# Reordering the opening of the first top-p attention: tile 0's logits through two PSUM names, its search ahead of a diffusion sum

## The chip, the cores and the metric

The kernel runs on one core of a Trainium2 chip. A core has five engines that run their own instruction streams[...]: TensorE (PE in the profile; PEld is its weight load), VectorE (DVE), ScalarE (ACT), GpSimd (POOL) and SyncE (SP), which here issues the DMAs. The metric is the device time of one execution in microseconds (us), the median over runs.

## The reference, cut to what matters

Four graph layers are applied in turn to `x`, 3327 nodes by 256 features, each followed by a residual and a normalization. The fourth is the one that the change touches. It runs two steps; each step computes a sparse attention from the current features and applies two operators:

```
q = X @ W1.T @ W2.T ;  k = X @ W3.T          # 64 features each
probs = softmax(q @ k.T)                      # N x N, row by row
A = probs, row-sparsified to the smallest set of largest entries whose
    sum reaches 0.9 (top-p), then divided by its row sum
R = (adj + I) / row sum
Xf = R @ Xf        # "diffusion"
Xa = A @ Xa        # "attention"
Z += Xf @ U1[n].T + Xa @ U2[n].T
```

For each row the kernel so needs: its 3327 logits, their exponentials and total, the threshold at which the sorted exponentials reach 0.9 of the total, and then two products with a 3328 x 3328 matrix.

## The kernel before, in words

Rows are padded to 3328 and cut into 26 tiles of 128 rows (`nt`). In the first attention (`p = 0`) tiles are worked in 13 pairs. Four things are made for each tile:

- **Logits**, `scores` (L1141): four groups (`c0` in steps of `KC` = 416). A group is two matmuls into a PSUM tile `sc` of two banks (L1148 to L1154), and a copy by ScalarE into `e`, the tile's 128 x 3328 row buffer (L1160; L1163 for the last group, whose halves differ in width). `sc` has one buffer, so a group's matmuls wait for the copy of the group before. The last column of `e` is filled by GpSimd (L1146).
- **Search**, `search_short` (L1387): VectorE takes the eight largest of each of 26 segments of `e` (MAX8 into `cand`), ranks them in six rounds (`top`, `rest`), ScalarE turns `e` into exponentials and their total (L1404) and later the 48 ranked ones (L1408), VectorE finds the threshold `v` and zeroes what lies below it in two halves of `e` (the two 128 x 1664 operations), and adds up what is kept (`kept`). It is a Python generator with 14 stops; `looks(k)` (L1688) advances the search at the head of a queue by `k` stops.
- **Diffusion sum**: tile 0's is made in layer 2; tile 1's by `diffused_first` (L1210): 26 matmuls of X against tiles `at` of the adjacency, which arrive in DMAs of 8, 8, 8 and 2 blocks (L1217), and one VectorE operation (`with_own`, L1207) that moves the sum out of PSUM into `F`. From tile 2 on, `diffused_pair` (L1224) makes two tiles at once with seven products in place of eight; each part of two column blocks needs three DMAs (L1230 to L1232) and one VectorE subtraction into `cb` (L1234). The buffers `at` are three.
- **Attention product**, `attended_pair` (L1252): TensorE transposes both tiles' `e` (`tp`), ScalarE copies them (`wt`, L1263), VectorE forms sums (`sw`), TensorE multiplies.

`own_part` (L1203) on GpSimd scales a tile's own rows before a diffusion sum is added. `blocks` (called at L1670) prepares differences of X in `G` with four VectorE operations at the beginning.

In this part `fixed` is true: TensorE's and VectorE's operations are kept in the order in which the Python code records them (helper at L891, which is why most lines of the profile read L891). ScalarE's, GpSimd's and SyncE's instructions are placed by the scheduler of the tile framework, and each engine then runs its own in that order. `stage` (L1692) interleaves the diffusion of a later pair with logits and looks; `attend_to` (L1706) finishes the queue of searches before a pair's transposes.

The beginning, ahead of the first `stage`, is what is changed:

```
groups = logits(0)
x = diffused_first(quads, psum, 1, xfs)
for _ in groups:
    next(x)
queue.append(searches[0])
spread = spreading(1)
groups = logits(1)
for _ in x:
    next(groups, None)
    looks(2)
```

So one group of tile 0's logits alternates with four products of tile 1's diffusion sum; then tile 0's search starts, with two looks for each further stop of the sum.

Of the kernel before, what the change touches and what calls it, by code (L numbers as in the profile page):

```python
# [9 lines left out]
F32 = mybir.dt.float32  # L10
# [8 lines left out]
P = 128  # L19
# [27 lines left out]
KC = 416  # L47
# [3 lines left out]
def gnn_kernel(ctx: ExitStack, tc: tile.TileContext, n: int, a: dict, out: bass.AP):  # L51
    nc = tc.nc
# [6 lines left out]
    small = ctx.enter_context(tc.tile_pool(name="small", bufs=4))  # L59
# [4 lines left out]
    eps_t = consts.tile([P, 1], F32, name="eps_t")  # L64
# [112 lines left out]
    with tc.tile_pool(name="l1b", bufs=1) as wpool, tc.tile_pool(name="l1at", bufs=2) as l1at:  # L177
# [62 lines left out]
        with tc.tile_pool(name="l1aw", bufs=1) as cwork, tc.tile_pool(name="l1c", bufs=2) as ch, \  # L240
# [61 lines left out]
            def plan(c):  # L302


                if c == 0:
                    return dict(project={g + 1: (g,) for g in range(NG)}, taps={7: (0,), 8: (1,), 9: (2, 3)}, gates={5: (0, 1), 6: (2,)},
                                silu=9, mixed=10, sizes={10: (0, 1), 11: (2, 3)}, exps=(11, 12), log=13)
                return dict(project={5: (0, 1), 6: (2, 3)}, taps={7: (0, 1), 8: (2, 3)}, gates={7: (0, 1), 8: (2, 3)},
                            silu=8, mixed=9, sizes={9: (0,), 10: (1, 2), 11: (3,)}, exps=(11, 12), log=13)
# [42 lines left out]
            banks = {0: ["y0", "y1", "y2", "ps"], 1: ["y3", "ps"]}  # L352
# [125 lines left out]
            def quota(c, s):  # L478


                k = c * DS + s
                n = next((x for x in range(2, nch) if k < due(x - 1)), None)
                if n is None:
                    return 24
                if k < due(0):
                    return 0
                if n not in shares:
                    busy = [duty(*divmod(i, DS)) for i in range(due(n - 2), due(n - 1))]
                    more = TILE * tiles_of(n)
                    level = max(busy) + more  # L490
                    while sum(max(0, level - x) for x in busy) > more:
                        level -= 1
                    shares[n] = [max(0, level - x) for x in busy]
                return TILE * starts[n] // P + sum(shares[n][:k - due(n - 2) + 1]) + AHEAD - taken
# [246 lines left out]
            for k, (c, s) in enumerate(states):  # L741
# [5 lines left out]
                p = plan(c)  # L747
# [55 lines left out]
                if c and 9 <= s < 9 + tiles_of(c - 1):  # L803
                    rs, nb = plus[:2]
                    i = s - 9
                    x = X[:, starts[c - 1] // P + i, :]
# [20 lines left out]
                q = quota(c, s)  # L827
# [38 lines left out]
    half = nt // 2 * P  # L866
    nseg = npad // SEG
    with tc.tile_pool(name="l3", bufs=1) as pool, tc.tile_pool(name="l3d", bufs=1, space=DRAM) as dram:
# [135 lines left out]
        with tc.tile_pool(name="l2c", bufs=1) as cpool:  # L1004
# [5 lines left out]
            with tc.tile_pool(name="l2a", bufs=1) as wpool, \  # L1010
                    tc.tile_pool(name="l2p", bufs=3, space=PSUM) as psum:

                q = cpool.tile([P, nt], F32, name="q")
# [124 lines left out]
        def in_order(op):  # L1138
            return lambda *x, **k: tc.keep_in_program_order(op(*x, **k))  # L1139

        def scores(work, psum, p, q, e):  # L1141


            copy = in_order(nc.scalar.copy) if p else nc.scalar.copy
            if npad > n:
                nc.gpsimd.memset(e[:, n:], NEG)  # L1146
            halves = e.rearrange("p (h c) -> p h c", h=2)
            for c0 in range(0, half, KC):  # L1148
                pl = psum.tile([P, 2, 512], F32, name="sc", bufs=1)
                ws = [min(KC, n - c0 - h * half) for h in range(2)]  # L1150

                for h, w in enumerate(ws):
                    k = slice(h * DA, (h + 1) * DA)
                    mm = tensor.matmul(pl[:, h, :w], q[k, :], kT[p][k, c0:c0 + w], start=True, stop=True)  # L1154
                    if p:
                        here(mm)
                if p:
                    yield
                if ws[0] == ws[1]:
                    copy(halves[:, :, c0:c0 + ws[0]], pl[:, :, :ws[0]])  # L1160
                else:
                    for h, w in enumerate(ws):
                        copy(halves[:, h, c0:c0 + w], pl[:, h, :w])  # L1163
                yield
# [45 lines left out]
        def diffused_first(quads, psum, it, out):  # L1210

            own_part(it)
            acc = psum.tile([P, 2, 512], F32, name="acc")[:, 0, :D]
            for j0 in range(0, nt, 4 * JQ):
                m = min(4 * JQ, nt - j0)
                at = quads.tile([P, 5, JQ, P], F32, name="at", bufs=3).rearrange("p k j r -> p (k j) r")
                nc.sync.dma_start(at[:, :m, :], a["adjT"][it][:, j0:j0 + m, :])  # L1217
                for j in range(m):
                    tensor.matmul(acc, at[:, j, :], X[:, j0 + j, :], start=(j0 + j == 0), stop=(j0 + j == nt - 1))
                    if j % 4 == 3 or j == m - 1:  # L1220
                        yield
            with_own(acc, it, out)

        def diffused_pair(quads, psum, i, b, out):  # L1224

            def part(j0):
                m = min(JQ, nh - j0)
                at = quads.tile([P, 5, JQ, P], F32, name="at", bufs=3)
                rows = [a["adjT"][2 * i + r].rearrange("p (h j) r -> p h j r", h=2)[:, :, j0:j0 + m, :] for r in range(2)]
                nc.sync.dma_start(at[:, :2, :m, :], rows[0])  # L1230
                nc.sync.dma_start(at[:, 2, :m, :], rows[1][:, 1])
                nc.sync.dma_start(at[:, 3:, :m, :], mixed[i][:, :, j0:j0 + m, :])  # L1232
                cb = quads.tile([P, 2, JQ, P], F32, name="cb", bufs=2)
                vector.tensor_tensor(cb[:, :, :m, :], at[:, 3:4, :m, :].to_broadcast([P, 2, m, P]), at[:, :3:2, :m, :], op=ALU.subtract)  # L1234
                a11, a12, a22, s2, s4, s1, s3 = (x[:, k, :m, :] for x, y in ((at, 5), (cb, 2)) for k in range(y))
                return a11, a12, s1, a22, s2, s3, s4

            for r in range(2):
                own_part(2 * i + r)
            pa = psum.tile([P, 2, 512], F32, name="acc")  # L1240
            ahead = part(0)
            yield
            for j0 in range(0, nh, JQ):
                w, ahead = ahead, part(j0 + JQ) if j0 + JQ < nh else None
                for j in range(min(JQ, nh - j0)):
                    products(pa, j0 + j, [x[:, j, :] for x in w], b)
                    yield
            c = assembled(quads, pa)
            for r in range(2):
                with_own(c[:, r, :], 2 * i + r, out)  # L1250
# [401 lines left out]
        with tc.tile_pool(name="l3w", bufs=2) as work, tc.tile_pool(name="l3s", bufs=4) as sm:  # L1652


            def start(p, t, es, searches, search):
                if p or t:
                    q = work.tile([2 * DA, P], F32, name="q")
                    nc.sync.dma_start(q, qd[p][t])
                else:
                    q = q0  # L1660
                es[t] = work.tile([P, npad], F32, name="e", bufs=4)
                searches[t] = search(work, sm, es[t], *(x[p][:, t:t + 1] for x in (tots, vs, kepts)),
                                     **({"halves": True} if p and t == nt - 1 else {}))
                return scores(work, psum, p, q, es[t])

            with tc.tile_pool(name="l3p", bufs=2, space=PSUM) as psum, tc.tile_pool(name="l3a", bufs=1) as quads:
                fixed = True
                es, searches, xfs, todo, queue = {}, {}, [xf0], [], []
# [3 lines left out]
                def look():  # L1672
                    while queue and next(queue[0], queue) is queue:
                        queue.pop(0)
# [5 lines left out]
                def logits(t):  # L1680
                    return start(0, t, es, searches, search_short) if t < nt else iter(())

                def spreading(i):
                    x = diffused_pair(quads, psum, i, b, xfs) if i < nh else iter(())
                    next(x, None)
                    return x

                def looks(k):  # L1688
                    for _ in range(k):
                        look()  # L1690
# [30 lines left out]
                        next(todo[r][0])  # L1721
                    ends[0] = todo[0][0]

                groups = logits(0)
                x = diffused_first(quads, psum, 1, xfs)
                for _ in groups:
                    next(x)
                queue.append(searches[0])
                spread = spreading(1)
                groups = logits(1)  # L1730
                for _ in x:
                    next(groups, None)
                    looks(2)
                for _ in groups:
                    pass
                queue.append(searches[1])
# [27 lines left out]
                for it in (nt - 2, nt - 1):  # L1764
                    for _ in range(7):
                        acc = next(values)
# [4 lines left out]
                    acc = next(values)  # L1771
# [19 lines left out]
            with tc.tile_pool(name="l3q", bufs=3, space=PSUM) as psum, tc.tile_pool(name="l3at", bufs=3) as atp, \  # L1791
                    tc.tile_pool(name="l3b", bufs=2) as lone:
                es, searches, xfs = {}, {}, []
# [4 lines left out]
                for i in range(-2, nt + 1):  # L1798
                    def search(t):
                        if 0 <= t < nt:  # L1800
                            next(searches[t])

                    values, logits = iter(()), iter(())
                    if 0 < i:
                        values = attended(lone, psum, es[i - 1], G, 3, in_order(nc.scalar.copy))
                    if i + 2 < nt:
                        logits = start(1, i + 2, es, searches, search_long)
# [196 lines left out]
```

## Time and profile before

| | |
|---|---|
| time, median of 3 runs | 3408.01 us (3407.56 to 3412.42) |
| the profiled execution's own time, and its span | 3412.8 us, 3411.0 us |
| PE, DVE, ACT, POOL busy over the span | 92%, 79%, 51%, 33% |
| layer 2's last product ends, first logits start | 1700.9 us, 1701.8 us |
| first transposes of the first pair complete | about 1758 us |
| stretch 1701 to 1757: PE, DVE, ACT, POOL busy | 35.95, 39.60, 17.43, 20.15 of 56 us |
| stretch 1757 to 2570 (rest of the first attention): PE busy | 795.56 of 813 us |

A row of the timeline gives start, duration, engine, line, operation, output and input tiles, the shapes, how many instructions are merged into it, and in brackets how long the engine had been idle before it and what ended the wait. A line L891 is the helper's, so rows are told apart by their tiles. An fp32 matmul of the program shows as two records, so "x8" is four matmuls. PEclk is the share of TensorE's full clock that was granted.

### The profile page before, as it was taken

What the parts mean: (1) busy time and instruction counts of PE and PEld (TensorE: products, weight loads), DVE (VectorE), ACT (ScalarE), POOL (GpSimd) and SP (SyncE); (2) the same over time, 40 slices, a digit from 0 to 9 for tenths busy, and PEclk for the clock granted to TensorE, in tenths of its full rate; (3) what the DMA queues carried; (4) which work ended last, traced back from release to release, by engine and by line L of the source; (5) the groups of instructions that cost most, each with busy time, mean ns of one, the idle gap of its engine ahead of it and who ended that gap; (6) DMA issues with size and microseconds to landing.
All of it is one profiled execution on the core that took longest, in us unless ns stands there. A gap on an engine that the chain in (4) does not pass through costs nothing. (4 is left out here: it accounts for less than half of the span.)

```text
span 3411.0 us, 50267 instructions
## 1 busy us (share of the span) xinstructions
PE 3129.6 (92%) x18301; PEld 2561.4 (75%) x18301; DVE 2687.8 (79%) x5899; ACT 1729.9 (51%) x2763; POOL 1132.1 (33%) x1328
## 2 busy tenths in 40 slices
PE   8999888988888766999989999999997899999997
PEld 5999656666676555888868888888885677777776
DVE  4665268999999997877578778878863889999996
ACT  1000556767667676111133333333336888888883
POOL 0000145656665654111310000000003566666663
PEclk9999998999999888999989999999998999999999
DMA  6775334434343221544322222323213122222221
GB/s 198 249 254 190 111 99 118 113 109 113 102 122 90 67 59 42 177 139 152 111 88 79 81 72 80 87 65 88 79 49 108 40 68 67 64 63 73 72 63 36
DMA packets 206263, 344.31 MB, mean 101 GB/s; under 512 B 22222, under 2 KB 129166, under 8 KB 205870
## 3 DMA queue, kind: packets, MB, share of 16 engines
q1 hardware_dynamic: 205998, 340.92, 33.8%
q8 instruction: 148, 2.42, 0.3%
q14 instruction: 117, 0.96, 0.1%
HBM read 304.65 MB, written 36.21 MB: 100 GB/s over the span
## 5 line engine op out<-in xcount | busy, mean ns | idle before, releaser
L330 POOL TENSOR_TENSOR h<-du,row 128x2048 f32<-128x2048 f32 (+1 forms) x110 | 465.9, 4236 | 344.6 <-DVE hc L330 249.8
L330 DVE TENSOR_TENSOR_SCAN h<-dA,carry,h 128x512 f32<-128x512 f32 (+1 forms) x384 | 448.9, 1220 | 18.2 <-ACT dA L337 18.1
L337 ACT ACTIVATE dA<-t,A_log 128x512 f32<-128x512 f32 (+1 forms) x448 | 292.6, 658 | 146.9 <-DVE h L330 145.2
L1296 PE MATMUL acc<-F,at 128*128 128x256 f32 x1352 | 343.9, 383 | 3.0 <-DMA at<-in_adjT 2.1
L1341 PE MATMUL acc<-G,wt 128*128 128x256 f32 x1352 | 333.0, 388 | 6.6 <-ACT wt L1139 6.3
L1079 PE MATMUL acc<-F,at 128*128 128x257 f32 x1352 | 303.4, 381 | 0.7 <-ACT r L1023 0.7
L389 PE MATMUL cb<-F,at 128*128 128x256 f32 x1196 | 294.7, 394 | 8.3 <-ACT hn L409 3.4
L1341 PEld LDWEIGHTS acc<-G,wt 128*128 128x128 f32 x1352 | 249.1, 191 | 62.6 <-ACT wt L1139 32.7
L1146 POOL MEMSET e<- 128x1 f32 x52 | 4.9, 99 | 835.2 <-PE tp L891 770.1
L1296 PEld LDWEIGHTS acc<-F,at 128*128 128x128 f32 x1352 | 240.7, 190 | 53.2 <-issue 21.5
L1079 PEld LDWEIGHTS acc<-F,at 128*128 128x128 f32 x1352 | 253.4, 190 | 36.3 <-issue 1.0
L680 PE MATMUL y<-ident,hc 128*128 128x128 f32 x1664 | 235.5, 295 | 46.9 <-DVE hc L330 46.8
L680 PEld LDWEIGHTS y<-ident,hc 128*128 128x128 f32 x1664 | 209.2, 153 | 88.8 <-DVE hc L330 63.9
L389 PEld LDWEIGHTS cb<-F,at 128*128 128x128 f32 x1196 | 229.4, 198 | 58.5 <-issue 19.6
L330 DVE TENSOR_TENSOR hc<-h,row 128x2048 f32<-128x2048 f32 (+2 forms) x114 | 242.9, 2133 | 11.4 <-PE y L680 4.3
L891 PE MATMUL acc<-X,at 128*128 128x128 f32 (+1 forms) x988 | 173.7, 287 | 6.1 <-issue 6.1
L1263 ACT COPY wt<-tp 128x512 f32<-128x512 f32 x156 | 90.8, 589 | 166.1 <-PE tp L891 152.8
L138 PE MATMUL acc<-t,cb 128*128 128x128 f32 (+1 forms) x1014 | 168.4, 275 | 0.0
L891 PEld LDWEIGHTS acc<-X,at 128*128 128x128 f32 x988 | 142.2, 193 | 30.2 <-issue 25.3
L891 PE MATMUL acc<-G,sw 128*128 128x128 f32 x936 | 155.5, 275 | 0.0
L891 DVE MAX8 cand<-e 128x8 f32<-128x128 f32 x676 | 139.8, 277 | 5.5 <-ACT e L1160 3.8
L1160 ACT COPY e<-sc 128x832 f32<-128x832 f32 x78 | 65.9, 845 | 149.4 <-PE sc L891 149.4
(417 smaller groups left out, 7274.2 us busy)
## 6 DMA issues: line engine op xcount, KB each, us to landing
at<-in_adjT SPq DMA_DIRECT2D x54, 832.0 KB, 4.5
at<-in_adjT SPq DMA_DIRECT2D x130, 320.0 KB, 3.0
row<-bc SPq DMA_DIRECT2D x80, 512.0 KB, 5.1
at<-in_adjT SPq DMA_DIRECT2D x52, 640.0 KB, 5.5
at<-in_adjT SPq DMA_DIRECT2D x52, 576.0 KB, 4.3
at<-in_adjT SPq DMA_DIRECT2D x72, 256.0 KB, 3.2
at<-mixed SPq DMA_DIRECT2D x72, 256.0 KB, 3.6
mixed<-cb SPq DMA_DIRECT2D x26, 640.0 KB, 4.2
```

The source lines that it names most:

```text
L138: mm = nc.tensor.matmul(acc, w[:, j, :], x, start=(y == 0 and k % 3 == 0 and k < 6), stop=(y == nh - 1 and k in (2, 6)))
L330: return lambda *x, **k: tc.keep_in_program_order(op(*x, **k))
L337: decays.append(op(*x, **k))
L389: ten.matmul(acc, at[:, j % JC, :], X0[:, j, :], start=(j == 0), stop=(j == nt - 1))
L680: x = ten.matmul(y[:, g * P:(g + 1) * P], h[:, g, i * P:(i + 1) * P], ident, is_transpose=True, start=(first and g == 0), stop=(last and g ...
L891: return lambda *x, **k: tc.keep_in_program_order(op(*x, **k))
L1079: nc.tensor.matmul(acc, at[:, j, :], F[:, j0 + j, :], start=(j0 + j == 0), stop=(j0 + j == nt - 1))
L1146: nc.gpsimd.memset(e[:, n:], NEG)
L1160: copy(halves[:, :, c0:c0 + ws[0]], pl[:, :, :ws[0]])
L1263: nc.scalar.copy(wts[-1], pt)
L1296: nc.tensor.matmul(acc, at[:, j, :], rhs[:, j0 + j, :], start=(j0 + j == 0), stop=(j0 + j == nt - 1))
L1341: tensor.matmul(acc, wt[:, j, :], rhs[:, j0 + j, :], start=(j0 + j == 0), stop=(j0 + j == nt - 1))
```

## The change

- `scores` takes a list of PSUM names and goes through it group by group. For tile 0 it is `("sc", "acc")`, so the second and fourth group use the two buffers of `acc`; for all others it stays `("sc",)`.
- A ScalarE copy of one column (`ex <- eps_t`) is recorded ahead of the first logits.
- All of tile 0's logits are recorded before the first product of tile 1's diffusion sum.
- `spreading(1)`, the start of the first pair's diffusion, moves behind that sum.
- In the loop over the sum, tile 1's logits advance at every second stop, and the search of tile 0 by three looks for each stop.

```
-        def scores(work, psum, p, q, e):
+        def scores(work, psum, p, q, e, banks=("sc",)):
...
-            for c0 in range(0, half, KC):
-                pl = psum.tile([P, 2, 512], F32, name="sc", bufs=1)
+            for k, c0 in enumerate(range(0, half, KC)):
+                bank = banks[k % len(banks)]
+                pl = psum.tile([P, 2, 512], F32, name=bank, bufs=1 if bank == "sc" else 2)
...
-                return scores(work, psum, p, q, es[t])
+                return scores(work, psum, p, q, es[t], ("sc", "acc") if not p and t == 0 else ("sc",))
...
-                groups = logits(0)
+                nc.scalar.copy(small.tile([P, 1], F32, name="ex"), eps_t)
                 x = diffused_first(quads, psum, 1, xfs)
-                for _ in groups:
-                    next(x)
+                for _ in logits(0):
+                    pass
                 queue.append(searches[0])
+                groups = logits(1)
+                for k, _ in enumerate(x):
+                    if k % 2 == 0:
+                        next(groups, None)
+                    looks(3)
                 spread = spreading(1)
-                groups = logits(1)
-                for _ in x:
-                    next(groups, None)
-                    looks(2)
```

## The prediction

> **What bounds the kernel now.** I read the page first (the first attention runs from about 1701 to 2570 us), then a table of stretches over it, then the waits at its beginning, then the timeline row by row. The table (length, PE, PEld, DVE, ACT, POOL busy, PEclk, DMA share, GB/s) gives the beginning and a steady pair of tiles:
>
> ```profile
> span 3411.0 us, 50267 instructions
> ...
> 1690.00:1752.00 62.00, 46.38 (x236) 33.11 (x234) 36.52 (x109) 18.63 (x25) 29.16 (x31) 0.92 0.35 102
> 1814.00:1876.00 62.00, 60.70 (x479) 53.94 (x478) 50.70 (x172) 23.28 (x39) 0.20 (x2) 1.00 0.26 75
> ```
>
> From 1814 on each 62 us (one pair) has PE busy 60.7: TensorE sets the pace, and what the beginning gains is kept. Between 1701 and 1757 PE is busy 36 of 56. The waits of PE and DVE there (total, times, longest):
>
> ```profile
> PE tp L891 <- DVE e L891: 10.3, 2, 9.0
> PE acc L891 <- issue: 6.1, 1, 6.1
> PE sc L891 <- ACT e L1160: 3.1, 2, 2.2
> DVE F L891 <- PE acc L891: 5.8, 1, 5.8
> ```
>
> The largest, 9.0 + 1.3, is the first pair's transposes waiting for tile 1's search. Followed backwards, that search starts at 1741.62, when tile 0's ends; and tile 0's stood 5.8 us behind the diffusion sum of tile 1. Timeline rows of that chain:
>
> ```profile
> 1694.00 26.13 POOL L1203 TENSOR_SCALAR F<-X,rdeg 128x256 f32<-128x256 f32 x23
> 1710.05 2.08 DVE L891 TENSOR_TENSOR G<-G,X 128x1664 f32<-128x1664 f32 x1
> 1720.07 0.19 POOL L1146 MEMSET e<- 128x1 f32 x4
> 1720.51 3.38 DVE L891 MAX8 cand<-e 128x8 f32<-128x128 f32 x17 [1.80 <-ACT e L1163]
> 1724.34 0.15 DVE L891 TENSOR_SCALAR neg<-top 128x1 f32<-128x1 f32 x1
> 1726.42 0.56 SPq L1230 DMA_DIRECT2D at<-in_adjT  x1
> 1727.68 0.83 ACT L1160 COPY e<-sc 128x832 f32<-128x832 f32 x1
> 1728.56 0.97 PE L891 MATMUL sc<-kT,q 64*128 64x416 f32 x4 [2.17 <-ACT e L1160]
> 1730.63 0.48 DVE L891 SCALAR_TENSOR_TENSOR F<-acc,rdeg,F 128x256 f32<-128x256 f32 x1 [5.79 <-PE acc L891]
> 1731.45 0.69 DVE L891 TENSOR_TENSOR cb<-at 128x512 f32<-128x512 f32 x1 [0.33 <-DMA at<-mixed]
> 1741.62 5.12 DVE L891 MAX8 cand<-e 128x8 f32<-128x128 f32 x26
> 1757.23 2.27 PE L891 MATMUL tp<-ident,e 128*128 128x128 f32 x9 [1.33 <-DVE e L891]
> ```
>
> And the clock at the restart (PE busy, PEclk, DMA share, GB/s): half until about 1762.
>
> ```profile
> 1750.00:1755.00 5.00, 0.00 (x0) 0.68 0.05 18
> 1755.00:1760.00 5.00, 3.22 (x14) 0.50 0.01 3
> 1760.00:1765.00 5.00, 5.00 (x33) 0.80 0.05 13
> ```
>
> [...] half clock from 1704.0 to 1714.2 and from 1751.7 to 1762.0, while the gaps of about 2.5 us near 1728 left it full. [...] the own-part rows on POOL take 0.93 us (median), but 2.2, 3.8 and 2.1 while the four G operations run (1704.35 to 1712.13); under MAX8 they stay at 0.92. [...]
>
> **The change, part by part.** Where instructions stand on each engine is read from the changed program as built.
>
> *Small copy.* The scheduler doesn't leave it where it is recorded: it stands in layer 1, behind the last decays (dA), and the table load still stands ahead of tile 0's first logits copy. So the load isn't sooner. Cost of a one-column ScalarE operation, by the 22 existing `ex` rows: 0.20 us. Between 0 and 0.2; I take 0, since that engine is busy 67% there and the scans behind it aren't queued on this copy.
>
> *Two PSUM names, logits in front.* First group at 1701.80 as before (0.97), the second right behind it. Table load to 1704.19, then copies of 0.85 each; the third group waits for the first copy (1705.06), the last copy ends near 1708.0 instead of 1720.9. But DVE is in G's preparation to 1712.13, so only then do the 26 MAX8 begin: 25 x 0.197 (5.12/26) ends at 1717.1. The 26th reads the filled column, and the fill on POOL is still queued behind the 23 own-parts, whose order the change leaves alone: 1720.07 + 0.10. A new wait of 3 us. Then `neg`: 0.65 behind the last MAX8 (1746.54 to 1747.19 in tile 1's search), 1720.85 instead of 1724.34. Of a 13 us earlier `e`, 3.5 us are left.
>
> *ScalarE's order.* Tile 1's second logits copy now stands behind tile 0's exponential (3.07). From `neg` to the matmuls that this copy releases took 4.22 (1724.34 to 1728.56): 1725.1. Queued behind that on PE: tile 1's third logits group and the last six products.
>
> *Diffusion sum.* Its DMA is issued behind one more (tile 1's q, about 0.35 us), so the first product is at 1709.2 instead of 1708.84. Twenty products at 0.465 (8 records in 1.86) and two groups at 0.9 make 11.05: 1720.3. Then 4.8 us of waiting, so the clock probably halves before 1725.1. Until the 24th product: group 0.9 + 4 x 0.465 = 2.76 at full, 5.5 at half clock; with the clock back some 4 us after the start, 4.9. So 1730.0, and the 26th at 1730.9 (1730.6 before).
>
> *Pair's start moved behind the sum.* Its three DMAs per part go behind the fourth `at`. Part one's buffer comes free with product 16 (1718.4), so it is in time. Part two's waits for product 24, at 1730.0. From the release to the subtraction on it took 1726.42 to 1731.4 = 5.0 before: 1735.0. That `cb` (0.69) now stands ahead of tile 1's MAX8: 1735.7. What covers this: tile 0's search ends 10.18 behind `neg` (1747.19 to 1757.37 in tile 1's), less the 0.6 of a `cb` inside it: 1730.4; F and the first `cb` to 1732.1. So DVE waits 2.9 us for the DMA, and ends 5.9 us ahead of before (1741.6). Were that DMA early, it would be 9.5.
>
> *Tile 1's search.* 1741.62 to 1757.37 = 15.75, so 1751.45: **5.9 us earlier**.
>
> *Restart.* PE's pair products in the meantime: two steps (1.56 each) on the first `cb`, two on the second, then the third `cb`, 8.1 behind the first MAX8 (1749.37 + 0.68 - 1741.62 = 8.4 at its end), at 1744.2; two steps and a logits group (4.1 at full, 6.2 in changing clock) end at 1748.3 to 1750.4. So PE idles under 3 us before the transposes, and mostly restarts at full clock. Before, restart to the end of the next logits group took 1757.23 to 1763.1 = 5.9, nearly all at half clock; at full clock, bound by ScalarE's three copies of 0.59, I make it 4.0. Gain 1.9, at 9 chances in 10: **1.7 us**.
>
> Other costs at nothing: the diffusion's PSUM tile waits for the second copy (1705.9), hidden by the DMA to 1709.2; 7 stops x 3 looks cover the search's 14, so no part of it is left behind the sum. Sum: 5.9 + 1.7 = 7.6 us, worked in the profiled execution (3411.0 span, 3412.8 in all, 4.8 above the median); as it is a difference, I take it from the median: 3408.0 - 7.6 = **3400.4**, own range 3398 to 3402.5.
>
> **The rivals.**
>
> *A: the filled column doesn't gate* (the fill comes by 1717). `neg` at 1717.9, the copy releases PE at 1722.1, PE waits 1.8 and keeps its clock, product 24 at 1724.9, second `cb` ends at 1730.6, search at 1746.4: 11 + 1.9 gives 3395. Against it: 23 own-parts of 26.13 us stand ahead of the fill unchanged; only the one slowed near 1712 could be shorter, by 0.6 at most.
>
> *B: the half clock holds longer.* Product 24 at 1730.6, restart at half clock again: 5.3 and nothing: 3402.7, within 0.2%. For it: three gaps of 3 to 5 us (1720, 1741, 1750) where there were fewer long ones.
>
> *C, slower: TensorE never gets its clock back in this stretch.* At half clock six pair steps and three logits groups take 2 x 12.3 = 24.6 from 1732, so PE, not the search, is late at the transposes (1756.6), and each later us at half clock loses 0.5: 3410 if it returns within 4 us of the restart. It decides from 1757 on; over 0.2% slower takes a half clock until about 1770. Against: after dense work it returned within 5.4 us at 1708.8 and 1757.2.
>
> *D: the shift is absorbed later*, 3408. Against: no row of the steady part waits for anything but these engines; PE waits for the search only 1.1 us per pair.
>
> **How the numbers follow.** Forecast 0.60, A 0.13, B 0.17, C 0.05, D 0.05. 0.2% is 6.8 us (below 3401.2), about what a measurement of this kernel can tell from no change. Of the forecast's range some 0.86 lies below that: 0.52, with A 0.65, and a little of B: faster 0.66. Within: the rest of the forecast, B, D: 0.29. Slower, C: 0.05. The range 3395 to 3404 takes in A's and B's centres; outside are C, D and the tails, 0.2.
>
> **What would show it.** Right: tile 0's last MAX8 starting just behind the fill at about 1720, some 3 us after the 25th; the second logits copy of tile 1 at 1724; DVE idle 2 to 4 us ahead of the second `cb`, released by a DMA; 26 MAX8 of tile 1 at about 1735.7; transposes complete near 1751.5; PEclk 1.00 there; from then 62.0 us per pair. Wrong: the fill elsewhere; no idle before that `cb`; half clock at the transposes; another period per pair.

## The result, and the profile after

The changed kernel takes 3404.02 us (median of 22 runs, 3394.49 to 3411.01) where the kernel before takes 3410.07 (22 runs beside it, 3405.20 to 3418.32). The ratio is 0.9981 with a 95% interval of 0.9974 to 0.9987. On 3410 us that is 6.5 us, between 4.4 and 8.9. The 0.2% of which the prediction speaks is 6.8 us, so the times leave open on which side of it the gain lies. A second set of the same program gave 0.9982 (0.9971 to 0.9993).

The profiled executions differ by more, 3411.0 against 3398.7 us of span, and not all of it belongs to the change. So I read each profile from one mark: the table load at the head of the first attention (1.28 us long, from 1702.91 us before, from 1697.14 changed; the 5.8 us between them arose ahead of the first logits, where the two programs' code differs by the one-column copy alone: over the fourteen profiles of this study the mark lies between 1693.3 and 1702.9 without that copy, between 1693.4 and 1706.3 with it). "Behind the mark" means from the start of that load. A second mark is the load of q that follows tile 2's last logits group, where the steady part begins: I call the distance between the two S. It is 60.34 us before and 51.13 changed.

The page's head, and the table of stretches over the beginning and a steady pair of the changed kernel (length, PE, PEld, DVE, ACT, POOL busy, PEclk, DMA share, GB/s):

```profile
span 3398.7 us, 50267 instructions
...
1684.40:1746.40 62.00, 48.89 (x254) 35.95 (x253) 42.50 (x122) 20.58 (x29) 29.32 (x31) 0.94 0.33 101
1799.10:1861.10 62.00, 60.70 (x478) 53.94 (x478) 50.71 (x171) 23.29 (x38) 0.20 (x2) 1.00 0.25 75
```

VectorE has 42.5 us of work in the first 62 where it had 36.5; the steady pair is the same to 0.01 us. The waits of the beginning (total, times, longest):

```profile
PE sc L891 <- ACT e L1161: 5.1, 2, 3.4
PE acc L891 <- DVE cb L891: 3.3, 2, 2.1
DVE cand L891 <- POOL e L1146: 2.3, 1, 2.3
DVE cb L891 <- DMA at<-mixed: 1.7, 1, 1.7
PE tp L891 <- DVE e L891: 1.2, 1, 1.2
```

The wait of 9.0 us for tile 1's search is down to 1.2, and VectorE's 5.8 us for the diffusion sum is gone. In their place stand the two new waits that the prediction named: 2.3 us for the filled column and 1.7 us for the DMA of the pair's second part. The rows of that chain in the timeline:

```profile
1707.46 4.92 DVE L891 MAX8 cand<-e 128x8 f32<-128x128 f32 x25
1714.57 0.18 POOL L1146 MEMSET e<- 128x1 f32 x4
1714.70 0.29 DVE L891 MAX8 cand<-e 128x8 f32<-128x128 f32 x1 [2.32 <-POOL e L1146]
1715.44 0.15 DVE L891 TENSOR_SCALAR neg<-top 128x1 f32<-128x1 f32 x1
1718.78 0.83 ACT L1161 COPY e<-sc 128x832 f32<-128x832 f32 x1
1719.66 0.97 PE L891 MATMUL sc<-kT,q 64*128 64x416 f32 x4 [3.45 <-ACT e L1161]
1722.58 0.55 SPq L1231 DMA_DIRECT2D at<-in_adjT  x1
1727.87 0.69 DVE L891 TENSOR_TENSOR cb<-at 128x512 f32<-128x512 f32 x1 [1.73 <-DMA at<-mixed]
1728.48 5.12 DVE L891 MAX8 cand<-e 128x8 f32<-128x128 f32 x26
1744.10 0.77 PE L891 MATMUL tp<-ident,e 128*128 128x128 f32 x5 [1.16 <-DVE e L891]
```

And the clock at the restart, which follows 1744.1 (same columns as above):

```profile
1744.00:1749.00 5.00, 4.66 (x35) 3.71 (x36) 4.35 (x14) 2.39 (x5) 0.00 (x0) 1.00 0.44 129
1749.00:1754.00 5.00, 5.00 (x48) 5.00 (x47) 3.38 (x14) 1.85 (x4) 0.00 (x0) 1.00 0.05 13
```

Full clock (1.00) from the first transpose. Nothing of this is lost on the way to the second attention: from the second mark to the first logits of the second attention it is 807.4 us in both profiles, and in the twelve others as well. There the profiles part again. The rows of the second attention's logits (count; least, median and most ns of one; first and last start), before, changed, and changed in another execution:

```profile
L1154 PE MATMUL sc<-kT,q x416: 508/612/1059, 2570.6 to 3308.9; 64*128 64x416 f32 x122, 64*128 64x415 f32 x17
```

```profile
L1155 PE MATMUL sc<-kT,q x416: 508/612/1060, 2555.7 to 3296.9; 64*128 64x416 f32 x122, 64*128 64x415 f32 x17
```

```profile
L1155 PE MATMUL sc<-kT,q x416: 508/612/1060, 2558.9 to 3302.3; 64*128 64x416 f32 x122, 64*128 64x415 f32 x17
```

738.3, 741.2 and 743.4 us for the same instructions. Over the fourteen profiles the distance is 738.1 to 743.5, and it doesn't go with the length of the beginning: 738.1 where S is 50.5, 743.5 where it is 46.6, 738.3 where it is 60.3, 742.1 where it is 59.7. So this part varies from execution to execution by 5 us, which is near the size of the whole effect; S, from one profile, is the sharper measure.

### The profile page after: what moved, and what is told of

It is laid out like the page before. It is cut to its first block, busy times and chain, and to the rows that moved or that the text cites. A ratio compares the mean times of both kernels' runs of the same rounds, so it can differ in the third digit from the quotient of the medians.

```text
span 3398.7 us, 50267 instructions
## 1 busy us (share of the span) xinstructions
PE 3121.9 (92%) x18301; PEld 2558.7 (75%) x18301; DVE 2689.5 (79%) x5899; ACT 1730.2 (51%) x2764; POOL 1127.6 (33%) x1328
## 5 line engine op out<-in xcount | busy, mean ns | idle before, releaser
L389 PEld LDWEIGHTS cb<-F,at 128*128 128x128 f32 x1196 | 230.7, 199 | 60.3 <-issue 20.1
L891 PEld LDWEIGHTS acc<-X,at 128*128 128x128 f32 x988 | 141.7, 193 | 25.8 <-issue 23.4
L138 PEld LDWEIGHTS acc<-t,cb 128*128 128x128 f32 x1014 | 140.3, 192 | 0.0
```

The lines of the kernel that those rows point to most:

```text
L138: mm = nc.tensor.matmul(acc, w[:, j, :], x, start=(y == 0 and k % 3 == 0 and k < 6), stop=(y == nh - 1 and k in (2, 6)))
L389: ten.matmul(acc, at[:, j % JC, :], X0[:, j, :], start=(j == 0), stop=(j == nt - 1))
```

## The experiments

The theory that I tested is the prediction's chain: fill on POOL, `neg`, exponential, second logits copy of tile 1, third logits group, product 24, DMA of the second part, second subtraction, tile 1's search, and then the clock at the restart. Its rivals: the two PSUM names carry the gain; the search ahead of the diffusion sum carries it alone; the clock makes the difference. The first table gathers all runs; times are us behind the mark, the fourth column is what the restart takes at full (4.0) or mostly at half clock (5.4 and more). Each row is one profile, and the changed kernel's own two differ by 2.6 us in S: a smaller difference between two rows says little by itself.

| kernel | tile 0's `neg` starts | tile 1's `kept` ends | from there to q's load | S | ratio to before (95%) |
|---|---|---|---|---|---|
| before | 21.43 | 54.46 | 5.88 | 60.34 | |
| changed | 18.30 | 47.10 | 4.03 | 51.13 | 0.9981 (0.9974 to 0.9987) |
| changed, again | 17.97 | 49.70 | 4.02 | 53.72 | 0.9982 (0.9971 to 0.9993) |
| looks alone | 21.32 | 47.69 | 4.02 | 51.71 | 0.9980 (0.9972 to 0.9989) |
| one bank | 17.74 | 46.45 | 4.03 | 50.48 | 0.9973 (0.9963 to 0.9983) |
| pair in place | 18.39 | 47.97 | 4.02 | 51.99 | 0.9987 (0.9978 to 0.9996) |
| no small copy | 17.74 | 48.20 | 4.02 | 52.22 | 0.9976 (0.9969 to 0.9983) |
| fill on VectorE | 14.95 | 43.87 | 4.03 | 47.90 | 0.9972 (0.9954 to 0.9990) |
| early part | 17.88 | 44.85 | 5.66 | 50.51 | 0.9964 (0.9950 to 0.9978) |
| fill and part | 15.03 | 42.02 | 5.53 | 47.55 | 0.9963 (0.9952 to 0.9975) |
| fill, part, warm | 15.57 | 42.55 | 4.03 | 46.58 | 0.9960 (0.9948 to 0.9973) |
| gap filled | 17.62 | 46.49 | 4.03 | 50.52 | 0.9978 (0.9969 to 0.9987) |
| before, warm | 21.27 | 54.26 | 5.42 | 59.68 | 1.0006 (0.9998 to 1.0013) |
| before, warm longer | 21.44 | 54.33 | 4.03 | 58.36 | 0.9996 (0.9987 to 1.0004) |

### Which part of the change carries the gain

**The search ahead of the sum, alone.** In the kernel before:

```diff
                 for _ in x:
                     next(groups, None)
-                    looks(2)
+                    looks(5)
```

> The kernel before, with looks(5) in place of looks(2): tile 0's whole search stands on VectorE ahead of tile 1's diffusion sum; logits, PSUM names and the pair's start as before. Theory (the stall behind the diffusion sum inside the search is the larger part, the logits in front the smaller): the exponential's neg stays at 21.4 us behind the table load, the search then runs through without the 5.8 us stall, tile 1's kept ends at 48.7 (54.5 before, 47.1 changed), S between 52.7 at full clock and 54.6 at half clock after the restart (60.3 before, 51.1 changed). Rival (the logits in front carry it): kept at 52.8 or later, S 58 or more.

Timeline of VectorE in that kernel, from `neg` on (mark at 1698.86):

```profile
1720.18 0.15 DVE L891 TENSOR_SCALAR neg<-top 128x1 f32<-128x1 f32 x1
...
1729.81 0.48 DVE L891 SCALAR_TENSOR_TENSOR F<-acc,rdeg,F 128x256 f32<-128x256 f32 x1
1730.20 0.68 DVE L891 TENSOR_TENSOR cb<-at 128x512 f32<-128x512 f32 x1
1730.80 5.12 DVE L891 MAX8 cand<-e 128x8 f32<-128x128 f32 x26
```

No row waits: the sum has long been ready when VectorE reaches it, and the second part's DMA has landed. `kept` ends at 47.69, a microsecond sooner than I had worked out (half of it because from `neg` to the end of tile 0's search takes 9.7 us when no subtraction stands inside it; I had used the 10.2 of a search that has one). One number in the source makes `kept` 6.8 us sooner, where the whole change makes it 7.4 sooner in its first profile and 4.8 in its second, and the time shows the same ratio. So the rival that the search ahead of the sum carries the gain by itself holds, and the one that the logits in front are needed for it falls. What the logits in front would bring without that search wasn't run.

**One PSUM name.** In the changed kernel:

```diff
-                return scores(work, psum, p, q, es[t], ("sc", "acc") if not p and t == 0 else ("sc",))
+                return scores(work, psum, p, q, es[t], ("sc",))
```

> The changed kernel with tile 0's logits in one PSUM name (sc) in place of two; the order of everything else as changed. Each group then waits for the copy before it. If the second name is worth nothing here: the last copy of tile 0 ends about 3 us later, still before VectorE is through with G, the first MAX8 starts when it did (10.3 us behind the table load), and S stays at 51.1. If the two names carry the gain: the search starts up to 3.6 us later and S is up to 54.7.

Timeline (mark at 1696.70), a group of tile 0 that waits for the copy before it, the last copy, and the third group of tile 1:

```profile
1698.90 1.76 PE L891 MATMUL sc<-kT,F 64*128 64x416 f32 x4 [2.35 <-ACT e L1161]
...
1706.12 0.91 ACT L1164 COPY e<-sc 128x416 f32<-128x416 f32 x2 [1.86 <-PE sc L891]
...
1718.66 0.97 PE L891 MATMUL sc<-kT,q 64*128 64x416 f32 x4 [0.27 <-ACT e L1161]
```

The last copy ends 10.3 us behind the mark and not 4.9. It costs nothing: VectorE is in G until 8.9 here and searches the columns in order. S is 50.48, 0.65 less than in the changed kernel's better profile (the fill came 0.55 us sooner). The logits were late enough, and at half clock, to push the diffusion sum back, so that TensorE's wait ahead of tile 1's third group is 0.27 us and not 3.45. No gain of the second name shows: what it makes ready early waits for G and for the fill.

**The pair's start back in its place.** In the changed kernel:

```diff
                 queue.append(searches[0])
+                spread = spreading(1)
                 groups = logits(1)
...
                     looks(3)
-                spread = spreading(1)
```

> The changed kernel, with the start of the first pair (its three DMAs, its first subtraction) back where the kernel before has it, ahead of tile 1's diffusion sum. Theory (this move is worth nothing by itself): the first product of the sum comes up to 1.7 us later, hidden by PE's later wait for a copy; the subtraction (0.7) stands ahead of the first MAX8, hidden by the fill; S within 0.7 of 51.1. Rival (the move is what lets the search of tile 1 start sooner): S 53 or more.

S is 51.99, 0.86 above the first profile of the changed kernel, a little outside the 0.7 but far from the rival's 53. The first product of the sum came at 10.6 us (6.4 changed), 2.5 us more than I had allowed. Between 51.1 and 53.7, where the changed kernel itself lies, this is no difference.

**Without the small copy.** In the changed kernel:

```diff
-                nc.scalar.copy(small.tile([P, 1], F32, name="ex"), eps_t)
                 x = diffused_first(quads, psum, 1, xfs)
```

> The changed kernel without the one-column ScalarE copy. Theory: the table load stands where it stood, right ahead of tile 0's first logits copy, and S is 51.1 within 0.7. Rival (the copy brings the table in sooner): the table load comes later against the first logits group and S grows by up to 1.3.

The table load stands where it stood, right ahead of the first copy, so the rival falls. S is 52.22, more than the 0.7 that I had allowed: VectorE waits 3.4 us for the second part's DMA, and TensorE's clock is at half after its gap of 4.58 us (PEclk 0.64 from 1723.98 to 1726.98). Nothing in the program differs there from the changed kernel. That led to the next pair of runs.

### The same program twice

The changed kernel was run and profiled again.

> The changed kernel once more, for the spread of the stretch between executions of one program. If the half clock windows fall as in the first profile, S is 51.1 and VectorE waits 1.7 us for the DMA of the second part; if one falls into PE's gap before tile 1's third logits group, as in the run without the small copy, the wait is about 3.4 us and S about 52.2. Total by the earlier runs: 3404, 6 us below the kernel before.

S is 53.72, outside even the upper case. The timeline of this second execution (mark at 1697.77), with the same rows as above:

```profile
1719.96 1.76 PE L891 MATMUL sc<-kT,q 64*128 64x416 f32 x4 [4.33 <-ACT e L1161]
...
1725.47 0.55 SPq L1231 DMA_DIRECT2D at<-in_adjT  x1
...
1731.11 0.69 DVE L891 TENSOR_TENSOR cb<-at 128x512 f32<-128x512 f32 x1 [3.11 <-DMA at<-mixed]
...
1731.72 5.12 DVE L891 MAX8 cand<-e 128x8 f32<-128x128 f32 x26
```

The third logits group starts at 22.2 us behind the mark, 0.3 sooner than in the first profile, but takes 1.76 us in place of 0.97: half clock. The DMA's release comes at 27.7 in place of 25.4, the second subtraction at 33.3 in place of 30.7. The clock around the two gaps, in stretches of 3.41 us. The first profile, clock full throughout:

```profile
1714.68:1718.09 3.41, 1.53 (x8) 1.00 (x6) 3.15 (x12) 2.38 (x1) 0.96 (x4) 1.00 0.52 136
1718.09:1721.50 3.41, 1.84 (x8) 1.17 (x9) 2.81 (x12) 2.68 (x5) 0.00 (x0) 1.00 0.19 61
1721.50:1724.91 3.41, 3.41 (x17) 2.15 (x16) 3.41 (x4) 0.58 (x3) 0.00 (x0) 1.00 0.22 63
```

The second:

```profile
1716.23:1719.64 3.41, 0.00 (x0) 0.00 (x0) 3.13 (x13) 3.41 (x3) 0.00 (x0) 1.00 0.46 141
1719.64:1723.05 3.41, 3.09 (x7) 1.68 (x8) 2.92 (x7) 1.46 (x3) 0.00 (x0) 0.50 0.02 5
1723.05:1726.46 3.41, 3.41 (x9) 2.70 (x8) 2.37 (x5) 0.00 (x0) 0.00 (x0) 0.50 0.00 0
1726.46:1729.87 3.41, 3.41 (x22) 2.24 (x22) 1.08 (x2) 0.91 (x2) 0.00 (x0) 1.00 0.73 194
```

In the first profile TensorE is busy for 1.53 and 1.84 us of the two stretches that the gap of 3.45 us touches, and PEclk is 1.00 in all four. In the second the gap of 4.33 us leaves one stretch without work, and the next two have 0.50. What makes the clock fall in the one and not in the other was not shown. The gap was shorter in the first profile because other half clock, from 7.3 to 10.7 us behind the mark (1704.43 to 1707.85), had slowed the first four products and the logits group behind them: 2.85 and 1.72 us, where they took 1.97 and 0.97 in the second.

**The gap filled.** To test that the half clock behind this gap makes the spread, 28 transposes of the identity were put into that gap of the changed kernel:

```diff
+                    if k == 4:
+                        idle = psum.tile([P, 4, P], F32, name="tp")
+                        for j in range(28):
+                            tensor.transpose(idle[:, j % 4, :], ident, ident)
                     if k % 2 == 0:
                         next(groups, None)
```

> The changed kernel with 28 transposes of the identity (3.1 us, read by nobody) on TensorE in its wait for the second copy of tile 1's logits, ahead of tile 1's third logits group. Two profiles of the changed kernel differ there: after a wait of 3.45 us the clock stayed full (S 51.1), after one of 4.33 us it was halved, the last products came 2.3 us later, VectorE waited 3.1 us in place of 1.7 for the second part's DMA, and S was 53.7. Theory (the half clock in this gap is the difference): PE's wait is 0.4 to 1.3 us, the clock stays full up to the pair's products, the second subtraction comes about 10.0 us behind the third logits group's start at most, kept ends at 46.2 to 47.1 behind the table load, S 50.3 to 51.1. Rival (the start of G or the DMAs differ): S spreads up to 53 as before.

Timeline (mark at 1706.28):

```profile
1723.60 3.22 PE L891 MATMUL tp<-ident 128*128 128x128 f32 x28
...
1728.12 0.97 PE L891 MATMUL sc<-kT,q 64*128 64x416 f32 x4 [1.30 <-ACT e L1161]
...
1736.41 0.69 DVE L891 TENSOR_TENSOR cb<-at 128x512 f32<-128x512 f32 x1 [1.81 <-DMA at<-mixed]
```

The group takes 0.97 (PEclk is 1.00 from the mark to 1745.28), VectorE waits 1.8 and not 3.1 or 3.4, S is 50.52: the theory's case. Counted from the start of tile 0's `neg`, so that G's start and the fill drop out, the second mark comes 32.9 us later here, 32.8 in the changed kernel's first profile and 35.7 in its second. It is one profile, so it shows what the filled gap brought here, not how often the unfilled kernel would have fallen the other way.

### The chain's two waits

**The fill on VectorE.** In the changed kernel, for tile 0 alone:

```diff
-                nc.gpsimd.memset(e[:, n:], NEG)
+                (vector if fixed and banks[-1] == "acc" else nc.gpsimd).memset(e[:, n:], NEG)
```

> The changed kernel, with the filled column of tile 0's e written by VectorE (behind the four G operations) and not by GpSimd behind its 23 own-parts. Measure S: from the table load of the first attention to the load of q that follows tile 2's last logits group (60.3 us before, 51.1 changed). If the chain fill, neg, exponential, second logits copy of tile 1 sets the stretch: the 26th MAX8 follows the 25th at once, neg 2.1 us sooner, PE's wait for that copy falls from 3.45 to about 1.3, S is 49.0 and the time 2.1 us below the changed kernel. If PE's products or the DMA of the pair's second part set it whatever the search does: neg is sooner, S stays at 51.1.

Timeline of VectorE (mark at 1693.41):

```profile
1708.36 0.15 DVE L891 TENSOR_SCALAR neg<-top 128x1 f32<-128x1 f32 x1
...
1720.92 0.69 DVE L891 TENSOR_TENSOR cb<-at 128x512 f32<-128x512 f32 x1 [1.85 <-DMA at<-mixed]
```

`neg` starts at 14.95 us, 3.4 sooner; 2.3 of it is the wait for the fill, the rest an earlier start of G in this execution (1.67 us behind the mark, 2.62 in the changed kernel's first profile). TensorE waits 1.59 us for the second copy, and S is 47.90, 3.2 less (the earlier start of G, 0.95, is in it). The DMA's wait stays (1.85 us), as it should: search and product 24 move together.

**The second part's buffer.** The last two blocks of the diffusion sum go into a buffer of `sw`:

```diff
-                at = quads.tile([P, 5, JQ, P], F32, name="at", bufs=3).rearrange("p k j r -> p (k j) r")
+                at = quads.tile([P, 4, P], F32, name="sw", bufs=3) if m <= 4 else quads.tile([P, 5, JQ, P], F32, name="at", bufs=3).rearrange("p k j r -> p (k j) r")
```

> The changed kernel, with the last two blocks of tile 1's diffusion sum loaded into a buffer of sw, which is idle then, so that the pair's second part gets the buffer that product 16 leaves and not the one that product 24 leaves. If product 24 sets when that DMA starts: the DMA is issued about 6 us sooner, VectorE's wait of 1.73 us before the second subtraction is gone, and S is 49.4 (51.1 changed). If VectorE or another buffer is late anyway: S stays at 51.1.

Timeline (mark at 1696.70): the DMA of the second part, both subtractions, and the first pair's transposes.

```profile
1712.05 0.55 SPq L1231 DMA_DIRECT2D at<-in_adjT  x1
...
1724.60 1.28 DVE L891 TENSOR_TENSOR cb<-at 128x512 f32<-128x512 f32 x2
...
1739.53 0.33 PE L891 MATMUL tp<-ident,e 128*128 128x128 f32 x1 [1.00 <-DVE e L891]
1741.41 0.77 PE L891 MATMUL tp<-ident,e 128*128 128x128 f32 x5 [1.55 <-DVE e L891]
```

The DMA is issued at 15.35 us (25.44 changed), the wait is gone, and `kept` ends at 44.85, 2.25 sooner: the 1.73 and a fill that came 0.4 sooner. But S is 50.51 and not 49.4. The restart took 5.66 in place of 4.03: with the subtractions on time TensorE runs through its pair products with 0.15 us of waiting, and then waits 1.0 and 1.55 us among the first transposes. In the 3 us from 1741.70 on PEclk is 0.66, in the next 3 it is 0.78. In this profile the clock so takes back 1.6 of the 2.25 us that the search gains. That isn't bound to happen: with the fill on VectorE the same two waits are 1.1 and 1.5 us, and PEclk is 1.00 there and behind them.

**Both.**

> The two edits before this one together. If both waits are in series on VectorE: no wait before the 26th MAX8 nor before the second subtraction, S is 51.1 - 2.1 - 1.7 = 47.3, and the time about 3.8 us below the changed kernel, 10 below the kernel before. If one hides behind the other: S is 49.0 to 49.4.

Timeline of VectorE (mark at 1697.62):

```profile
1707.30 4.91 DVE L891 MAX8 cand<-e 128x8 f32<-128x128 f32 x25
1712.65 0.15 DVE L891 TENSOR_SCALAR neg<-top 128x1 f32<-128x1 f32 x1
...
1722.69 1.28 DVE L891 TENSOR_TENSOR cb<-at 128x512 f32<-128x512 f32 x2
1723.89 5.12 DVE L891 MAX8 cand<-e 128x8 f32<-128x128 f32 x26
```

From the first G operation to the end of `kept` VectorE now has no wait for a fill or a transfer. `kept` ends at 42.02, 5.1 us sooner than in the changed kernel. S falls by 3.6 only, to 47.55, because of the clock at the restart (1739.64 on; the two waits are 1.0 and 1.5 us), as the table of stretches shows:

```profile
1739.00:1742.00 3.00, 2.26 (x12) 2.03 (x13) 2.71 (x9) 1.42 (x3) 0.00 (x0) 0.71 0.35 100
1742.00:1745.00 3.00, 3.00 (x17) 2.34 (x15) 2.04 (x6) 0.24 (x1) 0.00 (x0) 0.72 0.00 0
```

### The clock at the restart

**Before, with transposes of the identity ahead of the first pair's**, 64 at first:

```diff
                     finish()
+                    if i == 0:
+                        idle = psum.tile([P, 4, P], F32, name="tp")
+                        for k in range(64):
+                            tensor.transpose(idle[:, k % 4, :], ident, ident)
                     next(turned[0])
```

> The kernel before, with 64 transposes of the identity (read by nobody) on TensorE ahead of the first pair's transposes, to fill most of its 9 us of idling there. It prices the clock at the restart alone. Theory (the half clock costs 1.85 us there): kept of tile 1 stays at 54.5 us behind the table load, the transposes run at full clock, from kept to the load of q takes 4.0 in place of 5.9, S 58.5. Rival (ScalarE's copies bound the restart): 5.9 stays, S 60.3.

The 64 were too few: a transpose takes 0.11 us, so they were over after 7.15 us, and in the 4 us that followed TensorE had little work (0.30 us of the 3 from 1744 on); the clock was halved all the same (PEclk 0.66 and 0.77 in the two stretches of 3 us from 1747 on; restart 5.42). With 98:

> The kernel before with 98 transposes of the identity (11 us) ahead of the first pair's transposes, where 64 had ended 4 us too soon and the clock was halved all the same. If the half clock at the restart is worth what the changed kernel shows: kept of tile 1 stays at 54.4 us behind the table load, kept to the load of q takes 4.0 in place of 5.9, S 58.4 (60.3 before). If not: S 60.3.

```profile
1741.03 10.86 PE L891 MATMUL tp<-ident 128*128 128x128 f32 x98
...
1755.18 0.97 PE L891 MATMUL sc<-kT,q 64*128 64x416 f32 x4
```

`kept` ends at 54.33 as before, and the restart takes 4.03: 1.85 us, to the hundredth what the changed kernel has. The times can't show so little (0.9996, from 0.9987 to 1.0004).

**All together**: fill, early part, and 26 such transposes ahead of the first pair's.

> The changed kernel with tile 0's fill on VectorE and the last two blocks of the diffusion sum in sw's buffer, and with 26 transposes of the identity (2.9 us, read by nobody) on TensorE ahead of the first pair's transposes. Without them kept of tile 1 ended at 42.0 us behind the table load, but the restart ran at half clock and the load of q stood at 47.55: 5.5 after kept in place of 4.0. Theory (the clock takes back what the shorter search gains): kept stays at 42.0, restart at full clock, S 46.05, 1.5 us below the version without them. Rival (the copies of ScalarE bound the restart): S stays at 47.5.

The restart takes 4.03, S is 46.58 (`neg` came 0.5 us later in this execution than without the transposes). The time is 3396.54 us (6 runs, 3394.32 to 3402.09) beside 3411.01 for the kernel before: 0.9960, from 0.9948 to 0.9973. It beats the kernel before, and by the medians the changed kernel too: run beside it, the second set of the changed kernel has 3405.18; the intervals of the two ratios overlap by 0.0002. Between it and the version without the transposes (3397.99 us, 0.9963) the times don't decide.

## Why the prediction held, point by point

Its steps in the same frame: predicted, and measured in the changed kernel's two profiles (us behind the mark).

| step | predicted | first | second |
|---|---|---|---|
| last copy of tile 0's logits ends | 5.1 | 4.9 | 4.9 |
| first MAX8 of tile 0 | 9.2 | 10.3 | 9.1 |
| fill on POOL | 17.2 | 17.4 | 17.1 |
| `neg` | 17.9 | 18.3 | 18.0 |
| TensorE's wait for the second copy | 4.8 | 3.45 | 4.33 |
| clock after it | half | full | half |
| buffer of the second part released | 27.1 | 25.4 | 27.7 |
| from there to the second subtraction | 5.0 | 5.3 | 5.6 |
| VectorE's wait for it | 2.9 | 1.7 | 3.1 |
| tile 1's MAX8 | 32.8 | 31.3 | 33.9 |
| `kept` sooner than before | 5.9 | 7.4 | 4.8 |
| restart shorter than before | 1.7 | 1.85 | 1.86 |
| sum | 7.6 | 9.2 | 6.6 |

**The mechanism was right in each link**: the small copy brought no gain, the fill on POOL gated the 26th MAX8, and the DMA held by product 24 came last before the second subtraction. That only 3.5 of the 13 us are left was right as well: `neg` came 3.1 to 3.5 us sooner.

**What was mis-sized.** The step "the clock probably halves before 1725.1" was put as one outcome. It was the author's estimate, which the rows of before don't decide: there the clock stayed full (1.00) around a wait of 2.17 us and fell 5.3 us into the one of 8.96. It goes either way: the first profile kept its clock (product 24 1.7 us sooner than worked out), the second lost it (0.6 later). The working ahead of it took the first twenty products and two logits groups at full clock, 11.05 us; they took 11.07 in the second profile but 12.7 in the first, where 3.4 us of half clock fell on them, and it was this delay that made the wait 3.45 us and not 4.33. The 5.0 us from the buffer's release to the subtraction, taken over from the kernel before, were short by 0.3 and 0.6. They lie in the `mixed` DMA, which took 3.65 us from issue to landing before and 3.93 and 4.29 here; the third part's DMAs follow the second's by 1.9 us here and by 4.2 before, and whether that is the cause wasn't tested. One sum was slipped: by the rows F and the first subtraction take 1.2 us, so they would end at 1731.6 and the wait would be 3.4 us, not 2.9. The total isn't touched, since the DMA sets the start.

At the restart TensorE had stood still for 1.2 us in both profiles, less than the 3 of the prediction, and ran at full clock as forecast. Some 3.4 us of half clock had ended only 2.1 and 3.8 us earlier, and nothing in the working placed it. The restart at full clock (4.02 to 4.03 us) came in all eight profiles of the changed kernel and its variants (looks alone counted in) that leave the second part's buffer and the restart as they are.

**The time.** Predicted 3400.4, measured 3404.02: outside the forecast's own range (3398 to 3402.5) and at the very top of the wide one (3395 to 3404), so the number was met less well than the chain. Of the 3.6 us, 2.1 lie in the base, the median of three runs (3408.0) where 22 have 3410.1. The other 1.5 is a gain of 6.05 us by the medians (6.5 by the ratio) in place of 7.6; the ratio's interval, 4.4 to 8.9 us, takes in the 7.6, and the two profiles stand on either side of it.

**The rivals.** A (the fill doesn't gate) is refuted by the 2.3 and 3.2 us of wait for it; with the fill moved `neg` came 3.4 us sooner than in the first profile, 2.3 of it that wait. B (half clock longer, nothing gained at the restart) has its first half in the second profile, but the restart was at full clock in both. C didn't come. D (absorbed later) is refuted: 807.4 us from the second mark to the second attention in all fourteen profiles.

**What the prediction left out.** It took the parts of the change as one chain and didn't ask what the search ahead of the sum brings without the rest. The numbers were there: with `neg` left at 21.4, its own 9.6 of search and the rows' 1.2 of sum and subtraction give 32.2 for the start of tile 1's MAX8, no later than the 32.8 that it forecast for the whole change (31.9 measured). The logits in front make `neg` 3 us earlier, but the second part's buffer comes free later (25.4 and 27.7 us; 23.4 with the looks alone), and that hands the gain back as a wait of 1.7 to 3.1 us. The move of the pair's start isn't what costs it: with the start back in its place the buffer comes free at 26.1 and the wait is 3.1.

## What to carry to other kernels

When several edits act on one chain, work out the chain with each alone before adding them: here the search ahead of the sum alone brings as much as all the parts together, and none of the other three that were undone one by one (second PSUM name, pair's start, small copy) was shown to add to it. A gain on one engine has to be followed through the gaps that it opens on TensorE: with the early part alone the clock at the restart took back 1.6 of the 2.25 us that the search gained. A few useless matmuls in a gap price that directly: in the kernel before, 98 transposes brought 1.85 us at the restart. If executions of one program vary by as much as the effect, measure between two marks of the trace around the change and profile the same program twice.

## What the hardware showed that was not expected

The half clock came in stretches of very different length: 10.3 and 10.2 us in the kernel before (1703.98 to 1714.24 and 1751.77 to 1762.00), 3.4 us twice in the changed kernel's first profile (1704.43 to 1707.85 and 1738.58 to 1741.98), 6.8 us behind the gap of 4.33 in its second. The prediction judged the clock by the length of a wait: probably halved in one of 4.8 us, mostly full behind one under 3. The waits of TensorE in these profiles don't sort that way:

| profile | TensorE's wait | the clock |
|---|---|---|
| before | 0.91 and, behind 0.97 of work, 1.2 until the fall | half from 1703.98 |
| before | 2.17 (to 1728.56) | 1.00 from 1725 to 1730 |
| before | 8.96 (to 1755.45) | half from 1751.77 |
| changed | 2.50 (to 1703.51) | half from 1704.43 |
| changed | 3.45 (to 1719.66) | 1.00 |
| changed | 2.07 (to 1736.97) | half from 1738.58 |
| changed, again | 2.93 (to 1704.56) | 1.00 from 1703 to 1718 |
| changed, again | 4.33 (to 1719.96) | 0.50 in the 6.82 us from 1719.64 |
| no small copy | 4.58 (to 1721.94) | 0.64 from 1723.98 to 1726.98 |
| fill on VectorE | 1.09 (to 1735.36) and 1.48 (to 1737.14) | 1.00 |
| early part | 1.00 (to 1739.53) and 1.55 (to 1741.41) | 0.66 from 1741.70 to 1744.70 |

So waits of 2.50 and 2.07 us were followed by half clock where one of 3.45 in the same profile was not, and two pairs of nearly equal waits went different ways. What decides it was not shown.

The start of the four G operations, which wait for nothing that the trace names, lay between 0.8 and 2.6 us behind the mark in executions of nearly the same code. The fill on POOL started between 16.8 and 17.5 in the changed kernel and the variants that leave tile 0's fill there, and `neg`, which it gates, between 17.6 and 18.4: up to 0.8 us of the spread of S is from there.
